# Graph attention on one Trainium2 core: u as the loaded operand of the heads' products, the table's rows as the moving one

## The chip, the core and the metric

The kernel runs on one core of one Trainium2 chip. The metric is the device time of one execution in microseconds (us). Three runs of the kernel before gave 2905.03, 2912.14 and 2910.83 us; the median is 2910.83 us. One more execution was profiled: 2910.45 us, of which 2908.7 us lie between its first and last instruction (the span). All times of single instructions come from that execution. The engines are TensorE (PE, whose weight loads have a row of their own, PEld), VectorE (DVE), ScalarE (ACT), GpSimd (POOL) and SyncE (SP, which issues transfers).

## The reference

Four graph layers run one after the other on 4096 nodes with 256 features; each is x = x + layer(relu(layernorm(x))). Layer 0 is an attention diffusion, layer 1 a graph convolution, layer 2 graph attention with four heads, layer 3 a product with the adjacency. The change is in layer 2:

```python
def _L2_gnn_ref(H, A, W, a_l, a_r):          # H: (4096, 256), A: (4096, 4096), sparse
    mask = A + eye(n) > 0
    Wh = (H @ W.T).reshape(n, 4, 64)
    score_l = einsum('nhd,hd->nh', Wh, a_l)
    score_r = einsum('nhd,hd->nh', Wh, a_r)
    e = score_l[:, :, None] + score_r.T[None, :, :]
    e = where(e >= 0, e, 0.2 * e)
    e = where(mask[:, None, :], e, -inf)
    alpha = softmax(e, axis=2)
    out = einsum('nhm,mhd->nhd', alpha, Wh).reshape(n, 256)
    return elu(out)
```

Each node averages the 64 features of its neighbours for every head, with weights that are a softmax over the neighbours. The adjacency has about four other neighbours to a row besides the node itself.

## The kernel before

The nodes are cut into 32 blocks of 128 targets (NB = 32, P = 128). An earlier part of the kernel has found, for each block, which source nodes have an edge into it: four chunks (CHUNKS = 4) of up to 128 sources, and half a chunk more, so that two neighbouring blocks share one spare chunk of 128. The block's own 128 nodes are a fifth chunk.

The layer before attention writes a table of one row for each node, 264 numbers wide (TW). For each of the four heads it holds 65 numbers (DK + 1): the 64 features times exp(0.2 score_r), and that factor itself, whose sum is the softmax's denominator. The last four numbers are exp(0.8 score_r). A second small array, steep_d, holds exp(0.8 score_l) of the targets. The weight of an edge, up to a factor that the division takes out, is then max(exp(0.8 score_l) exp(0.8 score_r), 1).

The attention stage works on one block in each pass of the loop at L2456 (b counts the passes), and on four parts of different blocks at the same time:

- load(b), L2363: SP issues the targets' factors and the block's own table rows; POOL issues four indirect gathers of table rows (every second block one more for the spare chunk). The pool of the table rows has five buffers.
- entries(b, k), L2379: for chunk k, ACT (L2394) and in some cases DVE (L2396) multiply the four heads' target factors by the sources' factors, 128 x 128 each, and DVE (L2397) takes the maximum with 1 and multiplies by the mask. The result is u: sources in the partitions, targets along the free axis. u has two buffers.
- attend(b - 1, h), L2401: for head h, TensorE sums over the sources in six matmuls, five chunks of 128 sources and the spare half chunk of 64 (L2407 and L2415). Each fp32 matmul shows as two passes in the trace, each with a weight load. The loaded operand is the 65 columns of the table's rows, the moving operand is u with 128 columns. The sums come out in the PSUM tile acc with the 65 numbers in the partitions and the targets along the free axis.
- attended(b - 2), L2423, copies acc to SBUF (ACT, tile sums), and turned(b - 2), L2427, transposes it by four TensorE transposes into the PSUM tile po, now with the targets in the partitions. divided, risen and elu (L2432 to L2453) divide by the denominator, apply elu and add to x.

Six passes behind, class Projection (third) prepares layer 3 for block o = b - 6: normalise (ACT L2238, two transposes L2243 on TensorE), turned (DVE L2248), product (two fp32 matmuls L2254 with 256 moving columns) and store (ACT L2265, SP L2266).

The order of work on DVE, ACT and TensorE is written out by hand in the loop: the instructions of each of these engines run as the lines stand. On TensorE a pass is: attend(b - 1, 0), the four transposes of turned(b - 2), the two transposes of normalise(o), the product of o - 1, then attend(b - 1, 1), (b - 1, 2) and (b - 1, 3). When the last block has been attended, the passes that are left finish elu and layer 3's projection. Then comes a small check (L2508 writes its verdict) and the last layer, whose gathers wait for the table that L2266 stores.

Of the kernel before, what the change touches and what calls it, by code (L numbers as in the profile page):

```python
# [63 lines left out]
F32 = mybir.dt.float32  # L64
# [12 lines left out]
P = 128  # L77
# [5 lines left out]
HEADS = 4  # L83
DK = D // HEADS
# [581 lines left out]
def fast_layers(  # L666
# [21 lines left out]
    nc = tc.nc  # L688
# [18 lines left out]
    ident = const.tile([P, P], F32, name="ident")  # L707
# [188 lines left out]
    def spare_index(table, b):  # L896
        at = CHUNKS * NB + b // 2
        return table[:, at : at + 1]
# [15 lines left out]
    def side(b):  # L914
        return slice(b % 2 * (P // 2), (b % 2 + 1) * (P // 2))
# [13 lines left out]
    wk = layer0.enter_context(tc.tile_pool(name="wk", bufs=2))  # L929
    ps = layer0.enter_context(tc.tile_pool(name="ps", bufs=2, space=PSUM))  # L930
# [1266 lines left out]
    class Projection:  # L2197
# [48 lines left out]
        def turned(self, b):  # L2246
            ht = self.wk.tile([P, DC, P], F32, name="ht")
            nc.vector.tensor_copy(ht, self.tiles[b])  # L2248
            self.tiles[b] = ht
# [22 lines left out]
    with ExitStack() as st:  # L2272
        adj_pool = st.enter_context(tc.tile_pool(name="gcnadj", bufs=6))
        sm = st.enter_context(tc.tile_pool(name="gcnsm", bufs=4))
        wk = st.enter_context(tc.tile_pool(name="gcnwk", bufs=3))
        ps = st.enter_context(tc.tile_pool(name="gcnps", bufs=2, space=PSUM))
# [27 lines left out]
        with tc.manual_schedule(engines=MANUAL):  # L2304
            for b in range(NB + LAG + 3):
# [21 lines left out]
                if b < NB:  # L2327
                    acc = ps.tile([P, D], F32, name="acc")
# [24 lines left out]
    with ExitStack() as st:  # L2353
        tab_pool = st.enter_context(tc.tile_pool(name="gattab", bufs=5))
        u_pool = st.enter_context(tc.tile_pool(name="gatu", bufs=2))
        sm = st.enter_context(tc.tile_pool(name="gatsm", bufs=4))
        wk = st.enter_context(tc.tile_pool(name="gatwk", bufs=3))
        ps = st.enter_context(tc.tile_pool(name="gatps", bufs=2, space=PSUM))
        third = Projection(sm, wk, ps, w_last, to_table(wk, v_d[1]), 2)
        state = [{} for _ in range(NB)]  # L2360
        LAG = 6

        def load(b):  # L2363
            t = state[b]["targets"] = tab_pool.tile([P, HEADS, P], F32, name="targets")
            nc.sync.dma_start(t, steep_d[b : b + 1].to_broadcast([P, HEADS, P]))
            tab = state[b]["tab"] = tab_pool.tile([P, CHUNKS + 1, TW], F32, name="tabg")
            nc.sync.dma_start(tab[:, CHUNKS, :], table_d[b * P : (b + 1) * P, :])
            if b % 2 == 0:
                t = state[b]["targets_x"] = tab_pool.tile([P, HEADS, P], F32, name="targets_x", bufs=3)
                for r in range(2):  # L2370
                    nc.sync.dma_start(
                        t[side(r)], steep_d[b + r : b + r + 1].to_broadcast([P // 2, HEADS, P])
                    )
                state[b]["tab_x"] = tab_pool.tile([P, TW], F32, name="tabg_x", bufs=3)
                gather(state[b]["tab_x"], table_d, spare_index(column, b))
            for k in range(CHUNKS):
                gather(tab[:, k, :], table_d, main_index(column, k, b))

        def entries(b, k):  # L2379

            s = state[b]
            if k > CHUNKS:
                if b % 2:
                    return
                u = s["u_x"] = u_pool.tile([P, HEADS, P], F32, name="u_x")
                t, factors, mask = s["targets_x"], s["tab_x"], masks_x[:, b // 2 : b // 2 + 1, :]
            else:
                if k == 0:
                    s["u"] = u_pool.tile([P, CHUNKS + 1, HEADS, P], F32, name="u")
                u, t, factors, mask = s["u"][:, k], s["targets"], s["tab"][:, k], masks[:, b, k : k + 1, :]  # L2390
            for h in range(HEADS):
                by = factors[:, HW + h : HW + h + 1]
                if h < HEADS - 1 or k % 3 == 0:
                    nc.scalar.mul(u[:, h, :], t[:, h, :], by)  # L2394
                else:
                    nc.vector.tensor_scalar(u[:, h, :], t[:, h, :], by, None, op0=ALU.mult)  # L2396
            nc.vector.scalar_tensor_tensor(  # L2397
                u, u, 1.0, mask.to_broadcast([P, HEADS, P]), op0=ALU.max, op1=ALU.mult
            )

        def attend(b, h):  # L2401

            s = state[b]
            if h == 0:
                s["acc"] = ps.tile([DK + 1, HEADS, P], F32, name="acc")
            for k in range(CHUNKS + 1):
                nc.tensor.matmul(  # L2407
                    s["acc"][:, h, :],
                    s["tab"][:, k, h * (DK + 1) : (h + 1) * (DK + 1)],
                    s["u"][:, k, h, :],  # L2410
                    start=(k == 0),
                    stop=False,
                )
            shared = state[b - b % 2]
            nc.tensor.matmul(  # L2415
                s["acc"][:, h, :],
                shared["tab_x"][side(b), h * (DK + 1) : (h + 1) * (DK + 1)],
                shared["u_x"][side(b), h, :],
                start=False,
                stop=True,  # L2420
            )

        def attended(b):  # L2423
            t = state[b]["sums"] = wk.tile([DK + 1, HEADS, P], F32, name="sums")
            nc.scalar.copy(t, state[b]["acc"])

        def turned(b):  # L2427
            po = state[b]["po"] = ps.tile([P, HEADS, DK + 1], F32, name="po")
            for h in range(HEADS):
                nc.tensor.transpose(po[:, h, :], state[b]["sums"][:, h, :], ident[: DK + 1, : DK + 1])  # L2430

        def divided(b):  # L2432
            s = state[b]
            rden = sm.tile([P, HEADS, 1], F32, name="rden")
            nc.vector.reciprocal(rden, s["po"][:, :, DK:])
            s["y"] = wk.tile([P, HEADS, DK], F32, name="y")
            nc.vector.tensor_tensor(
                s["y"], s["po"][:, :, :DK], rden.to_broadcast([P, HEADS, DK]), op=ALU.mult
            )

        def risen(b):
            s = state[b]
            s["below"] = wk.tile([P, D], F32, name="below")
            nc.scalar.activation(s["below"], s["y"].rearrange("p h d -> p (h d)"), AF.Exp)

        def elu(b):

            s, xo = state[b], xr[:, b, :]
            y = s["y"].rearrange("p h d -> p (h d)")
            below = s["below"]  # L2450
            nc.vector.scalar_tensor_tensor(xo, y, 0.0, xo, op0=ALU.max, op1=ALU.add)
            nc.vector.scalar_tensor_tensor(xo, below, 1.0, xo, op0=ALU.min, op1=ALU.add)
            third.stats(b)  # L2453

        with tc.manual_schedule(engines=MANUAL):
            for b in range(NB + LAG + 2):  # L2456
                o = b - LAG
                entered, summed, turning, ended = (0 <= b - k < NB for k in range(4))
                if entered:
                    load(b)  # L2460
                if turning:
                    attended(b - 2)
                if summed:
                    attend(b - 1, 0)
                if turning:
                    turned(b - 2)
                if 0 <= o < NB:
                    third.normalise(o)
                if 0 <= o - 1 < NB:
                    third.product(o - 1)  # L2470
                if ended:
                    elu(b - 3)
                if entered:
                    entries(b, 0)
                    entries(b, 1)
                if 0 <= o < NB:
                    third.turned(o)
                if summed:
                    attend(b - 1, 1)
                    attend(b - 1, 2)  # L2480
                if entered:
                    entries(b, 2)
                if turning:
                    divided(b - 2)
                if 0 <= o + 1 < NB:
                    third.shifts(o + 1)
                if entered:
                    for k in range(3, CHUNKS + 2):
                        entries(b, k)
                if turning:  # L2490
                    risen(b - 2)
                if 0 <= o - 2 < NB:
                    third.store(o - 2)
                if summed:
                    attend(b - 1, 3)
# [16 lines left out]
    with ExitStack() as st:  # L2512
        adj_pool = st.enter_context(tc.tile_pool(name="lastadj", bufs=6))
        wk = st.enter_context(tc.tile_pool(name="lastwk", bufs=3))
        ps = st.enter_context(tc.tile_pool(name="lastps", bufs=2, space=PSUM))
        for b in range(NB):
# [7 lines left out]
            acc = ps.tile([P, D], F32, name="acc")  # L2524
# [69 lines left out]
```

## Time and profile before

| what | us |
|---|---|
| runs of the kernel, median (lowest to highest) | 2910.83 (2905.03 to 2912.14) |
| the profiled execution | 2910.45 |
| its span | 2908.7 |
| first and last matmul pass of the attention heads (start) | 2454.6 and 2702.9 |
| verdict stored, last layer's first load (start) | 2714.7 and 2715.8 |
| passes of L2407 and L2415, all blocks | 1280 and 256 |

In the whole span PE is busy 2523.0 us, DVE 2312.7, ACT 1976.6 and POOL 1098.0. These are sums over stages that have different limits, so what matters here is the stretch from 2454 to 2715 us. The profile also gives the clock that TensorE was granted; it is either full or half, and changes in steps of 3.41 us. Its mean over the span is 0.921.

### The profile page before, as it was taken

The numbers are of one execution on the slowest core, as the hardware profiler recorded it, in microseconds if no ns is written. First come the engines' busy times: TensorE is split into PE (matmuls) and PEld (weight loads), VectorE is DVE, ScalarE is ACT, GpSimd is POOL, SyncE is SP. The second block draws the span as 40 slices with busy tenths as digits, with TensorE's granted clock in tenths as the row PEclk, the third lists the DMA queues.
The fourth block names the chain that finished last, engine by engine and source line by source line (L and its number), as shares of the span: only waits on it lengthen the run. The fifth ranks groups of instructions, "written<-read, shape, count | busy, mean of one in ns | idle before, by whom it ended". The sixth has DMA issues, their size and how long they took to land. (4 is left out here: it accounts for less than half of the span.)

```text
span 2908.7 us, 43850 instructions
## 1 busy us (share of the span) xinstructions
PE 2523.0 (87%) x12359; PEld 1850.5 (64%) x12359; DVE 2312.7 (80%) x9516; ACT 1976.6 (68%) x3289; POOL 1098.0 (38%) x1152
## 2 busy tenths in 40 slices
PE   5769999999999884699999999999895776999777
PEld 4537777777777762467676766677773554788444
DVE  4799999999999866898989879999964765888200
ACT  2689999999999634887888878788520123999100
POOL 3200000000000001488888554344425752764476
PEclk7779999999999996899999999999996887999887
DMA  7611222222222113244444433334337653654576
GB/s 254 222 55 59 92 69 87 89 69 91 80 75 89 40 40 103 64 126 126 122 136 118 134 111 102 99 117 123 101 98 227 209 165 104 173 164 121 160 210 183
DMA packets 227371, 349.57 MB, mean 120 GB/s; under 512 B 34727, under 2 KB 160172, under 8 KB 227116
## 3 DMA queue, kind: packets, MB, share of 16 engines
q1 hardware_dynamic: 185820, 237.70, 25.7%
q0 software_dynamic: 40320, 108.72, 13.6%
q8 instruction: 101, 1.65, 0.2%
q14 instruction: 154, 1.26, 0.1%
q10 hardware_dynamic: 976, 0.23, 0.0%
HBM read 280.22 MB, written 66.28 MB: 119 GB/s over the span
## 5 line engine op out<-in xcount | busy, mean ns | idle before, releaser
L1269 ACT ACTIVATE unread<-e,next_pair 128x4096 uint8<-128x4096 f32 (+1 forms) x320 | 859.5, 2686 | 160.9 <-DVE next_pair L1365 109.0
L1619 PE MATMUL pa<-va,at 128*128 128x256 f32 x2048 | 495.2, 387 | 0.0
L1619 PE MATMUL pa<-h,at 128*128 128x256 f32 x2048 | 469.0, 379 | 0.1
L1619 PEld LDWEIGHTS pa<-va,at 128*128 128x128 f32 x2048 | 376.4, 193 | 65.4 <-issue 21.6
L1619 PEld LDWEIGHTS pa<-h,at 128*128 128x128 f32 x2048 | 376.6, 190 | 45.3 <-issue 0.5
L1483 DVE MAX8 best<-near 128x8 f32<-128x256 f32 x1024 | 394.6, 415 | 0.1
L1610 ACT COPY at<-pat 128x512 f32<-128x512 f32 x512 | 284.0, 577 | 135.3 <-PE pat L1604 135.1
L1236 PE MATMUL pl<-kt,qb 64*128 64x512 f32 x1024 | 280.4, 657 | 91.3 <-ACT e L1250 88.4
L1604 PE MATMUL pat<-ident,e 128*128 128x128 f32 x2048 | 305.0, 279 | 51.2 <-DVEq L1543 25.1
L1604 PEld LDWEIGHTS pat<-ident,e 128*128 128x128 f32 x2048 | 240.0, 142 | 139.1 <-DVEq L1543 47.8
L1485 POOL COPY eighth<-best 128x16 f32<-128x16 f32 x64 | 47.1, 736 | 722.7 <-DVE best L1483 711.7
L1250 ACT ACTIVATE e<-pl,minus_guess 128x1024 f32<-128x1024 f32 x256 | 284.3, 1125 | 26.8 <-PE pl L1236 26.7
L1475 DVE SCALAR_TENSOR_TENSOR near<-e,end_hi 128x4096 f32<-128x4096 f32 x64 | 286.6, 4477 | 0.1
L1535 DVE SCALAR_TENSOR_TENSOR e<-e,end_t 128x4096 f32<-128x4096 f32 x64 | 286.2, 4472 | 0.2 <-issue 0.2
L889 POOL DMA_INDIRECT vg<-v_d,column x256 | 243.4, 951 | 91.0 <-issue 67.7
L920 PE MATMUL acc<-vg,ac 128*128 128x256 f32 x640 | 215.9, 489 | 66.3 <-DMA vg<-v_d,column 29.6
L920 PEld LDWEIGHTS acc<-vg,ac 128*128 128x128 f32 x640 | 146.9, 247 | 132.1 <-issue 59.8
L1236 PEld LDWEIGHTS pl<-kt,qb 64*128 64x128 f32 x1024 | 89.8, 194 | 195.7 <-ACT e L1250 156.4
L889 POOL DMA_INDIRECT vg<-mixed_d,column x128 | 180.5, 1410 | 57.6 <-issue 32.4
L2407 PE MATMUL acc<-u,tabg 128*65 128x128 f32 x1280 | 170.2, 280 | 13.5 <-DVE u L2397 13.5
L889 POOL DMA_INDIRECT vg<-far_d,column x128 | 166.6, 1301 | 39.0 <-issue 38.1
L2394 ACT ACTIVATE u<-targets,tabg 128x128 f32<-128x128 f32 x544 | 162.1, 389 | 10.0 <-DMA targets_x<-steep_d 10.0
(608 smaller groups left out, 4427.7 us busy)
## 6 DMA issues: line engine op xcount, KB each, us to landing
adj<-in_adjt SPq DMA_DIRECT2D x128, 512.0 KB
ac<-adjc_d SPq DMA_DIRECT2D x64, 320.0 KB
adjc_d<-ac SPq DMA_DIRECT2D x32, 320.0 KB
vg<-v_d SPq DMA_DIRECT2D x64, 128.0 KB
targets<-steep_d SPq DMA_DIRECT2D x32, 256.0 KB
ac<-adjc_d SPq DMA_DIRECT2D x32, 256.0 KB
table_d<-tab SPq DMA_DIRECT2D x32, 132.0 KB
tabg<-table_d SPq DMA_DIRECT2D x32, 132.0 KB
```

Source lines behind the costliest of these rows:

```text
L889: nc.gpsimd.indirect_dma_start(out, None, rows, bass.IndirectOffsetOnAxis(ap=index, axis=0))
L920: nc.tensor.matmul(acc, ac[:, k, :], v[:, k, :], start=(k == 0), stop=False)
L1236: nc.tensor.matmul(pl[:, r, :], s["qb"][rows], kt[rows, j * 512 : (j + 1) * 512], start=True, stop=True,)
L1250: nc.scalar.activation(s["e"][:, j * 1024 : (j + 1) * 1024], pl.rearrange("p r c -> p (r c)"), AF.Exp, bias=minus_guess[:, b : b + 1], acc ...
L1269: nc.scalar.activation(unread[:, :width], s["e"][:, :width], func, bias=s["at"], scale=-1.0, accum_out=s["signs"] if func == AF.Sign else ...
L1475: nc.vector.scalar_tensor_tensor(near, s["e"], end["hi"][:, b : b + 1], s["e"], op0=ALU.is_lt, op1=ALU.mult, accum_out=s["low"])
L1483: nc.vector.max(best[:, k, :], near[:, k * (N // SEG) : (k + 1) * (N // SEG)])
L1535: nc.vector.scalar_tensor_tensor(s["e"], s["e"], last, s["e"], op0=ALU.is_ge, op1=ALU.mult, accum_out=s["held"])
L1604: nc.tensor.transpose(pt[:, k, :], s["e"][:, c * P : (c + 1) * P], ident)
L1610: nc.scalar.copy(at, s["pt", g])
L1619: nc.tensor.matmul(s["pa"], s["at", g][:, k, :], va[:, c, :D], start=(c == 0), stop=(c == NB - 1))
L2407: nc.tensor.matmul(s["acc"][:, h, :], s["tab"][:, k, h * (DK + 1) : (h + 1) * (DK + 1)], s["u"][:, k, h, :], start=(k == 0), stop=False,)
```

## The change

The two operands of the six matmuls change places. u is loaded (128 columns) and the table's rows move (65 columns), so the sums come out in po with the targets in the partitions. The copy attended and the four transposes turned are dropped, with the tiles acc and sums.

```diff
             if h == 0:
-                s["acc"] = ps.tile([DK + 1, HEADS, P], F32, name="acc")
+                s["po"] = ps.tile([P, HEADS, DK + 1], F32, name="po")
+            cols = slice(h * (DK + 1), (h + 1) * (DK + 1))
             for k in range(CHUNKS + 1):
                 nc.tensor.matmul(
-                    s["acc"][:, h, :],
-                    s["tab"][:, k, h * (DK + 1) : (h + 1) * (DK + 1)],
-                    s["u"][:, k, h, :],
-                    start=(k == 0),
-                    stop=False,
+                    s["po"][:, h, :], s["u"][:, k, h, :], s["tab"][:, k, cols], start=(k == 0), stop=False
                 )
             shared = state[b - b % 2]
             nc.tensor.matmul(
-                s["acc"][:, h, :],
-                shared["tab_x"][side(b), h * (DK + 1) : (h + 1) * (DK + 1)],
-                shared["u_x"][side(b), h, :],
-                start=False,
-                stop=True,
-            )
-
-        def attended(b):
-            t = state[b]["sums"] = wk.tile([DK + 1, HEADS, P], F32, name="sums")
-            nc.scalar.copy(t, state[b]["acc"])
-
-        def turned(b):
-            po = state[b]["po"] = ps.tile([P, HEADS, DK + 1], F32, name="po")
-            for h in range(HEADS):
-                nc.tensor.transpose(po[:, h, :], state[b]["sums"][:, h, :], ident[: DK + 1, : DK + 1])
+                s["po"][:, h, :], shared["u_x"][side(b), h, :], shared["tab_x"][side(b), cols], start=False, stop=True
+            )
...
                 if entered:
                     load(b)
-                if turning:
-                    attended(b - 2)
                 if summed:
                     attend(b - 1, 0)
-                if turning:
-                    turned(b - 2)
```

## The prediction

> **What bounds the kernel now.** I read the busy table of the stage first, then the instructions of one loop pass, then the rows that price the new operand order, last the granted clock. The stretches of 40 us in the middle of the attention stage show which engine sets the pace (columns: stretch, length, busy us and count of PE, PEld, DVE, ACT, POOL, then clock, DMA share, GB/s):
>
> ```profile
> 2520.00:2560.00 40.00, 40.00 (x302) 32.24 (x301) 34.76 (x89) 36.21 (x117) 26.59 (x27) 1.00 0.62 174
> 2560.00:2600.00 40.00, 40.00 (x303) 32.05 (x302) 35.30 (x89) 37.05 (x120) 25.56 (x27) 1.00 0.58 166
> ```
>
> PE has no idle time and the full clock. Over 2470 to 2690 us DVE is busy 194.2 and ACT 201.0 of 220 us. The transposes of L2430 start 7.72 us apart in this stretch, so a block costs PE 7.72, DVE 6.81, ACT 7.05 us. PE is the bound, the others are near.
>
> The timeline shows what PE does (start, length, engine, line):
>
> ```profile
> 2565.67 0.46 PE L2430 MATMUL po<-ident,sums 65*128 65x65 f32 x4
> 2565.97 0.39 PE L2243 MATMUL pt<-ident,h 128*128 128x128 f32 x2
> 2566.19 1.03 PE L2254 MATMUL pv<-w_last,ht 128*128 128x256 f32 x4
> ...
> 2568.60 1.07 PEld L2407 LDWEIGHTS acc<-u,tabg 128*65 128x65 f32 x10 [0.17 <-issue]
> 2568.60 1.31 PE L2407 MATMUL acc<-u,tabg 128*65 128x128 f32 x10
> ...
> 2569.84 0.19 PEld L2415 LDWEIGHTS acc<-u_x,tabg_x 64*65 64x65 f32 x2 [0.17 <-issue]
> 2569.84 0.43 PE L2415 MATMUL acc<-u_x,tabg_x 64*65 64x128 f32 x2
> ```
>
> A head is ten passes of 128 source rows and two of 64; at each change between them the next load waits 0.17 us. From 2568.60 to 2570.20 a head costs 1.594 us, four cost 6.38; the transposes add 0.25 (2573.39 to 2573.64, before L2243 follows), L2243 and L2254 the rest.
>
> **What is removed.** Per block 0.25 us of transposes on PE, inside the bound: gain 0.25. The 0.17 us wait ahead of them stays, since L2243 now follows the 64-row passes. The ACT copy (582 ns, L2425) lies beside PE: nothing while PE is the bound (0.58 a block if ACT were), and ACT falls to 6.47 us a block. No engine waits on a new thing: po is written one loop pass earlier than it is divided, as acc was. On SP only the order of two loads in the stage's first blocks is exchanged; nothing is added to any queue.
>
> **What the swap costs at full clock.** Loads and passes exchange sizes: 128 columns loaded, 65 moved. The rows that price it:
>
> ```profile
> 2574.78 1.25 PE L2407 MATMUL acc<-u,tabg 128*65 128x128 f32 x10
> 63.79 0.97 PEld L1051 LDWEIGHTS pst<-halves,near 128*128 128x128 f32 x8
> 125.06 1.62 PEld L1051 LDWEIGHTS pst<-halves,near 128*128 128x128 f32 x7 [0.52 <-issue]
> 2573.39 0.33 PEld L2430 LDWEIGHTS po<-ident,sums 65*128 65x128 f32 x4 [0.17 <-issue]
> ```
>
> The first: ten passes with 128 moving columns, (1.25 - 0.272) / 9 = 0.109 us each; the load of 65 hides. L1051 loads 128 fp32 columns and moves two: at full clock (0.97 - 0.19) / 7 = 0.111 us, at half clock (1.62 - 0.333) / 6 = 0.2145. So the load alone then sets the pace, and the new passes, of the same load and 65 moving columns (half of 0.107 us), cost 0.111 each, not half. The low bound is the last row, 0.063 us a pass with 128 columns loaded and 65 moved, but in a transposition, one pass instead of two, whose load is shorter (L2243 shows the same 0.143 us as here; an fp32 load of 128 columns shows 0.190). The high bound is load and move in turn, 0.111 + 0.054. I take L1051, since it has the very load. The restart after each change of rows keeps its length: load 0.107 instead of 0.054, pass 0.054 instead of 0.107. Head: ten follow-on passes at +0.0025 plus some ns at the two restarts, about +0.034 us; four heads +0.14. Net at full clock 0.14 - 0.25 = -0.11 us a block.
>
> **What it costs through the clock.** Here is the decisive term. Windows on the 3.41 us grid on which the clock changes:
>
> ```profile
> 123.65:127.07 3.42, 3.42 (x11) 2.39 (x11) 2.98 (x11) 3.12 (x6) 0.00 (x0) 0.50 0.50 181
> 127.07:130.48 3.41, 3.41 (x11) 2.38 (x11) 2.85 (x22) 1.86 (x4) 0.00 (x0) 0.50 0.47 154
> 1113.52:1116.93 3.41, 3.23 (x21) 2.13 (x19) 1.83 (x8) 0.14 (x1) 0.00 (x0) 1.00 0.63 205
> 1116.93:1120.35 3.42, 0.00 (x0) 0.00 (x0) 3.08 (x12) 0.00 (x0) 0.00 (x0) 0.50 1.00 201
> 2458.37:2461.79 3.42, 3.03 (x12) 2.31 (x13) 2.86 (x8) 3.42 (x13) 2.50 (x4) 0.50 0.69 167
> 2461.79:2465.20 3.41, 3.41 (x16) 2.56 (x14) 2.11 (x4) 1.61 (x6) 2.80 (x3) 0.50 0.62 182
> 2465.20:2468.61 3.41, 3.41 (x26) 2.63 (x26) 0.00 (x0) 1.25 (x4) 2.49 (x4) 1.00 0.54 147
> ```
>
> The first two have PE busy throughout, half of it in L1051's loads, and the clock stays at half. The third has PE busy 3.23 us with sixteen two-column passes, and the clock falls behind it. So neither busy time nor loads count. I added up, for every window of the trace, the share in which columns move (0.107 us for 128 at full clock, 0.213 at half). At full clock it fell after every window below 0.37 and after none above 0.44; at half it rose after none below 0.74 and after all above 0.86. In the stage itself, 2458.37 holds 11 moving passes of 0.213 (0.71) and stays, 2461.79 about 14 (0.88) and releases the full clock.
>
> The stage begins at half clock and will be left there: a new pass moves 0.108 of each 0.2145 us, a share of 0.51 at best and 0.44 with the changes of rows. Half-clock heads cost as much as now by the same exchange of sizes: 2460.06 to 2463.00 = 2.94 us. Not before layer 3's matmuls start, behind attend(6, 0), is there more that moves: two transposes of 0.213 and four passes of 0.427, 2.13 us in one piece. A window that holds this piece and 1.28 us of heads reaches (2.13 + 1.28 x 0.5) / 3.41 = 0.81, between the bounds; a block offers such a window with a chance of (3.41 - 2.13) / 3.41 = 0.38. I take one block until the clock rises, with none and all as ends.
>
> At full clock a window inside the heads has a share of 12 x 0.054 / 1.628 = 0.40, again between the bounds. There, windows with 6 to 8 passes lost the clock 21 times in 28, those with 10 or more kept it three times in three; as if each pass counted some ns more than its columns. A new window holds 25 passes, so I take it that the clock is kept, with its loss as the rival.
>
> [...]
>
> **The sum.** (1) From 2465.65 to 2503.9, the start of the sixth group of transposes, are 22 heads at full clock now, 38.25 us; at half they take 22 x 2.94 = 64.7: +26.4. POOL, ACT and DVE have slack there. (2) One block more with layer 3's matmuls at half clock: 4 x 2.94 + 2.13 = 13.9 against 7.72: +6.2. (3) 24 blocks at full clock: -2.7. (4) The tail: after the last head PE waits 0.97 us for the copy and runs the transposes, at the head of the chain that reaches 2714.7; without them about -1.2. Sum +28.7, on the profiled execution's 2910.45 (0.4 below the median): **2939 us**. With no or four blocks in (2) it is 2933 to 2958; with the 5 us by which the runs of before differ, the forecast's own range is 2928 to 2963.
>
> ```profile
> 2703.30 0.58 ACT L2425 COPY sums<-acc 65x512 f32<-65x512 f32 x1 [3.82 <-PE acc L2415]
> 2703.93 0.33 PEld L2430 LDWEIGHTS po<-ident,sums 65*128 65x128 f32 x4 [0.97 <-ACT sums L2425]
> ```
>
> **Rivals.** A, the clock does not last: windows inside the heads at 0.40 lose it and most of the stage runs at half. For it: the 21 of 28. Against: the windows with many passes. If never regained: 26.4 + 25 x 6.2 + some 5 for a tail at half clock = +186, 3097; with a quarter of the blocks at full clock some 40 less, 3055. About 3075.
> B, the clock is as now (busy time decides): -0.11 x 30 - 1.2 = -4.6, 2906. Against it: the windows above.
> C, faster: loads of 128 columns partly hide, passes near L2430's 0.063, and the clock comes as now. PE falls by 48 x 0.046 = 2.2 us to below DVE, which then sets 6.81 + 0.05: -0.86 x 30 - 1.2 = -27, 2883. It decides once a pass costs under 0.092 us (PE at DVE's 6.85). Against: L1051 in both clocks.
>
> **How the numbers follow.** Forecast 0.55, A 0.25, B 0.12, C 0.08. The first two hold 0.8, so the range runs from 2925 to 3100; B and C are left out. Changes under 0.3% (8.7 us) can't be told from none: slower 0.80, same 0.11 (B), faster 0.09 (C and B's lower end).
>
> **What would show it.** Passes of the heads start 0.111 us apart at full and 0.2145 at half clock; the granted clock is half from 2454 until layer 3's matmuls run, some 2530 to 2545, then full. If the clock is full by 2466, term (1) falls; if it keeps changing after 2545, A holds; if passes stand 0.06 to 0.09 apart, the load was mispriced.

## The result, and the profile after

The changed kernel takes 3067.73 us (3062.09 to 3068.87) against 2911.05 us: 1.0539 times the kernel before, with a 95% interval of 1.0519 to 1.0558. The profiled execution has a span of 3066.2 us against 2908.7, 157.5 us more.

The place is the attention stage alone. From the first to the last matmul pass of the heads it takes 409.6 us (2450.7 to 2860.2) instead of 248.4. The stage starts 3.9 us earlier for reasons that lie ahead of it (in a second trace of the kernel before it starts 9.3 us earlier with the same code), and the last layer takes 194.0 us in both: 161.2 - 3.9 + 0.2 behind the heads = 157.5.

Busy time of the changed kernel in 40 us stretches of the stage (columns as in the prediction):

```profile
2580.00:2620.00 40.00, 40.00 (x160) 36.32 (x159) 20.32 (x51) 18.74 (x61) 13.94 (x15) 0.50 0.36 101
2700.00:2740.00 40.00, 40.00 (x237) 36.23 (x237) 28.70 (x71) 30.49 (x100) 21.47 (x23) 0.80 0.52 144
2780.00:2820.00 40.00, 40.00 (x157) 36.08 (x158) 19.02 (x49) 18.24 (x60) 8.37 (x10) 0.50 0.17 47
```

PE is busy all the time, as before, but at a granted clock of 0.50, and its passes in 40 us have fallen from 302 to 160. DVE and ACT have fallen from about 35 to 20 us. From 2500 to 2690 us the trace puts 70.3 us of DVE's waits for u down to ACT and names nothing for 94.4 us of ACT's; that both wait in the end for PE to free one of the two buffers of u is inferred, from PE alone having no idle time. A reader who looks at busy shares alone would see no difference on PE. The chain that ended last, from the page of the changed kernel, agrees:

```profile
PE 15%; POOL 2%; DMA 2%; issue 1%; DVE 0%; ACT 0%; POOLq 0%; SPq 0%; ACTq 0%; DVEq 0%
```

The chain on the page of the kernel before (PE 1%) can be followed back only to 2707 us, behind the heads; now it runs through the heads' passes. Their timeline, at half clock and at full clock:

```profile
2573.69 2.39 PE L2408 MATMUL po<-tabg,u 128*128 128x65 f32 x10
2576.02 0.69 PE L2412 MATMUL po<-tabg_x,u_x 64*128 64x65 f32 x2
2576.63 2.39 PE L2408 MATMUL po<-tabg,u 128*128 128x65 f32 x10
...
2704.98 1.33 PE L2408 MATMUL po<-tabg,u 128*128 128x65 f32 x10
2706.24 0.43 PE L2412 MATMUL po<-tabg_x,u_x 64*128 64x65 f32 x2
2706.60 1.33 PE L2408 MATMUL po<-tabg,u 128*128 128x65 f32 x10
2704.98 1.19 PEld L2408 LDWEIGHTS po<-tabg,u 128*128 128x128 f32 x10
```

A head costs 2.94 us at half clock and 1.62 at full clock. The loads at full clock are (1.19 - 0.19) / 9 = 0.111 us apart: a pass moves half the columns and takes as long as before (0.109 us), so by these rows the load sets the pace (in the runs below with 72, 80 and 128 moved columns and the same load the passes of a train start 0.111 to 0.112 us apart too). What makes the difference is how long each clock lasts. I take the distance from one block's first 64-row pass to the next block's (differences are taken before rounding):

| block distances | after, us | before, us | difference |
|---|---|---|---|
| 6 without layer 3's matmuls, half clock | 70.9 | 44.1 | +26.8 |
| 20 with them, all at half clock, 13.79 each | 275.9 | 154.5 | +121.3 |
| 3 in which the clock changes (9.71, 10.74, 11.01) | 31.5 | 23.2 | +8.3 |
| 2 at full clock, 7.53 each | 15.1 | 15.5 | -0.4 |
| behind the last of these, to the start of the last head's last pass | 11.1 | 6.3 | +4.8 |

So at full clock the new order was a little faster (7.53 against 7.72), but only two whole blocks had it. In this trace, as in that of the kernel before, every stretch of full or of half clock is a whole number of 3.413 us long. Windows of the changed kernel on that grid show how the full clock comes and goes:

```profile
2526.23:2529.64 3.41, 3.41 (x13) 2.81 (x12) 2.14 (x5) 2.78 (x10) 2.59 (x3) 0.50 0.85 223
2693.48:2696.89 3.41, 3.41 (x15) 3.06 (x13) 3.06 (x9) 2.23 (x7) 2.07 (x3) 0.50 0.69 198
2696.89:2700.31 3.42, 3.42 (x26) 3.10 (x25) 1.89 (x6) 0.00 (x0) 0.00 (x0) 1.00 0.13 37
...
2713.96:2717.37 3.41, 3.41 (x27) 3.07 (x26) 2.75 (x7) 2.07 (x8) 1.74 (x2) 1.00 0.46 129
2717.37:2720.79 3.42, 3.42 (x14) 3.06 (x13) 3.18 (x9) 3.42 (x13) 2.73 (x3) 0.50 0.85 212
2720.79:2724.20 3.41, 3.41 (x27) 3.14 (x27) 3.06 (x8) 1.76 (x6) 0.84 (x2) 1.00 0.21 59
2724.20:2727.61 3.41, 3.41 (x16) 3.17 (x15) 1.57 (x5) 2.64 (x10) 1.67 (x2) 0.50 0.40 116
```

The third number from the end is the clock of the window. I added up the share in which columns move, as in the prediction. It is an estimate from the distance of passes in this trace: at full clock passes of 512 columns start 0.429 us apart (L1646), which is 0.107 for 128, and at half clock passes of 256 start 0.427 apart (L2254), 0.213 for 128. The first window has 0.76 and is not followed by full clock; the second has 0.76 too and is. The third (0.40) keeps it, 2713.96 (0.40) loses it, 2717.37 (0.80, with layer 3's matmuls) is followed by one window at full clock, and 2720.79 (0.40) loses it again. PE is busy in all of them.

### The profile page after: what moved, and what is told of

The parts are those of the page before. It is cut to its first block, busy times and chain, and to the rows that moved or that the text cites. A ratio compares the mean times of both kernels' runs of the same rounds, so it can differ in the third digit from the quotient of the medians.

```text
span 3066.2 us, 43621 instructions
## 1 busy us (share of the span) xinstructions
PE 2675.4 (87%) x12231; PEld 2019.6 (66%) x12231; DVE 2316.1 (76%) x9516; ACT 1964.5 (64%) x3257; POOL 1088.4 (35%) x1152
## 5 line engine op out<-in xcount | busy, mean ns | idle before, releaser
L2408 PE MATMUL po<-tabg,u 128*128 128x65 f32 x1280 | 286.8, 403 | 13.5 <-DVE u L2397 13.5
L1485 POOL COPY eighth<-best 128x16 f32<-128x16 f32 x64 | 40.3, 630 | 724.2 <-DVE best L1483 713.2
L2408 PEld LDWEIGHTS po<-tabg,u 128*128 128x128 f32 x1280 | 271.4, 313 | 30.1 <-issue 12.4
L2397 DVE SCALAR_TENSOR_TENSOR u<-u,masks 128x512 f32<-128x512 f32 x160 | 110.7, 692 | 156.1 <-ACT u L2394 134.7
```

The costliest lines, as they stand in the source:

```text
L2408: nc.tensor.matmul(s["po"][:, h, :], s["u"][:, k, h, :], s["tab"][:, k, cols], start=(k == 0), stop=False)
```

## The experiments

The theory after the result: in this kernel the granted clock follows the share of time in which columns move through PE, as estimated above. 65 columns behind a load of 128 give 0.40 inside the heads at full clock, behind which it was lost at 2717.37 and 2724.20 us (and kept at 2700.31), and 0.44 at half clock, behind which no window of the stage rose to full. The main rival: the new operand order is slow in itself, by its loads or because a head's work has grown. The first four runs fell on a chip on which the kernel before took 3129.16 us (other stages are slower there: the attention stage's gathers begin at 2612.0 us in the run with 128 columns, at 2445.9 in the trace of the kernel before), the others on chips with 2911 us; each ratio is to the kernel before on its own chip.

**128 columns moved.** Of the table's rows 128 columns are moved where 65 are needed; the other sums are overwritten or not read.

```diff
+        MOVED = 128
...
-                s["po"] = ps.tile([P, HEADS, DK + 1], F32, name="po")
-            cols = slice(h * (DK + 1), (h + 1) * (DK + 1))
+                s["po"] = ps.tile([P, HEADS, P], F32, name="po")
+            low = min(h * (DK + 1), TW - MOVED)
+            to = h * P + low - h * (DK + 1)
+            sums = s["po"].rearrange("p h d -> p (h d)")[:, to : to + MOVED]
+            cols = slice(low, low + MOVED)
...
```

The matmuls then write `sums`.

> The operands stand as in the changed kernel (u loaded, 128 columns), but each pass moves 128 columns of the table's rows instead of 65; the other 63 sums are thrown away. Loads, number of passes and everything else stay. Theory (the granted clock follows the share of time in which columns move): at half clock a head moves 12 x 0.213 of 2.95 us, 0.87, so full clock is granted at some 2465 us as in the kernel before, a pass stays at 0.111 us because the load sets the pace, a block costs 7.53 us, and the time is 2900 to 2912 us although more work is done. Rival (the new order is slow in itself, by its longer loads, or PE work counts): 3068 us or more, half clock in most of the stage.

Measured: 1.0018 (0.9999 to 1.0038) instead of 1.0539, some 4 us of 2911 above what was expected. The first full clock, from 2631.2 us, was lost at 2638.0, when PE had almost nothing to do (a share of 0.06); the second lasted from 2658.5 us to the end of the stage. Nearly twice the moved columns with the same loads takes the loss away (1.0018 instead of 1.0539): the rival falls. A block took 7.9 us and not the 7.53 that I expected. The heads show where the time is:

```profile
2700.36 1.38 PE L2413 MATMUL po<-tabg,u 128*128 128x128 f32 x10
2701.67 0.49 PE L2415 MATMUL po<-tabg_x,u_x 64*128 64x128 f32 x2
2702.08 1.38 PE L2413 MATMUL po<-tabg,u 128*128 128x128 f32 x10
```

A head is 1.72 us instead of 1.62. Inside the trains the passes still start 0.111 to 0.112 us apart; what has grown lies at the changes of rows, with 1.31 us instead of 1.26 from the first of the ten passes to the first of the two, and 0.41 instead of 0.36 from there to the next ten. My reading, an estimate from these four distances: at each change the load of 128 and the pass of 128 both stand open, where the two kernels have one long and one short.

**80 columns moved** (the same edit with MOVED = 80).

> As the run with 128 moved columns, but with 80. Theory: at full clock a window inside the heads has a share of 12 x 0.0667 / 1.63 = 0.49, above the 0.44 over which the clock was never lost in the kernel before, so once full it stays full; at half clock the heads alone have 0.55 and cannot raise it, a window that holds layer 3's matmuls whole reaches 0.85 and can. So half clock up to 2530 us and some blocks more, then full to the end: 2935 to 2965 us, the course that my forecast described for 65 columns. Rival (a clock once low stays low in this operand order): about 3068 us.

Measured: 1.0079 (1.0050 to 1.0107), some 23 us of 2911 and just below the range expected. Busy time in this run (its stage begins later, on the slower chip):

```profile
2680.00:2720.00 40.00, 40.00 (x158) 35.91 (x158) 20.43 (x52) 19.96 (x64) 15.36 (x17) 0.50 0.33 90
2720.00:2760.00 40.00, 40.00 (x285) 36.08 (x284) 33.10 (x86) 32.07 (x105) 23.50 (x24) 1.00 0.57 153
2760.00:2800.00 40.00, 40.00 (x285) 36.02 (x284) 34.79 (x89) 34.36 (x112) 25.14 (x26) 1.00 0.59 167
```

This is the course that I had forecast for 65 columns: half clock until layer 3's matmuls have run for some two blocks, then one rise at 2719.9 us, and full clock to the end of the stage, with blocks of 7.6 us.

**A warm start.** Five matmuls of 512 moving columns behind the first head, results unused:

```diff
                 if summed:
                     attend(b - 1, 0)
+                if b == 1:
+                    spare = ps.tile([P, 512], F32, name="spare", bufs=1)
+                    for _ in range(5):
+                        nc.tensor.matmul(spare, ident, xr[:, 0:2, :].rearrange("p b d -> p (b d)"), start=True, stop=True)
```

> The changed kernel (65 moved columns) with five more fp32 matmuls of 512 moving columns behind the first head, whose result is not used; they take 6 to 9 us and raise the clock to full before the heads begin. It parts the two steps of my forecast: is the clock kept in the heads (my forecast), or lost in windows with a share of 0.40 (rival A of the prediction)? Kept: full clock from 2465 us to the end of the stage, about 2906 + 8 = 2914 us. Lost: full clock for one to six windows, then half until layer 3's matmuls or longer, 3045 to 3080 us.

Measured: 1.0519 (1.0479 to 1.0558). The clock rose at 2628.2 us and was lost at 2635.0. This is not quite the test that I meant. The window before the loss:

```profile
2631.58:2634.99 3.41, 2.82 (x20) 2.30 (x19) 1.13 (x3) 0.00 (x0) 2.80 (x3) 1.00 0.35 89
2634.99:2638.40 3.41, 0.54 (x2) 0.57 (x2) 0.69 (x1) 0.00 (x0) 2.66 (x3) 0.50 0.52 132
```

PE had run ahead and stood idle, with a share of 0.30; ACT had nothing to multiply, and POOL was still issuing gathers. Four later losses in this run are clean: the clock came back for one window each at 2792.0, 2802.2, 2979.7 and 2990.0 us and was lost after shares of 0.40, with PE busy throughout. The run with 65 columns further down repeats the question without the filler.

**128 columns, in pairs.** Heads 0 and 1, and 2 and 3, have their 64-row matmuls side by side:

```diff
...
-                    attend(b - 1, 0)
+                    attend_chunks(b - 1, 0, True, False)
...
-                    attend(b - 1, 1)
-                    attend(b - 1, 2)
+                    attend_spare(b - 1, 0, False, True)
+                    attend_spare(b - 1, 1, True, False)
+                    attend_chunks(b - 1, 1, False, True)
+                    attend_chunks(b - 1, 2, True, False)
+                    attend_spare(b - 1, 2, False, True)
...
-                    attend(b - 1, 3)
+                    attend_spare(b - 1, 3, True, False)
+                    attend_chunks(b - 1, 3, False, True)
```

Here attend_chunks holds the ten passes of 128 rows of a head and attend_spare the two of 64.

> As the run with 128 moved columns, and the 64-row matmuls of two heads stand side by side (heads 0 and 1, heads 2 and 3), so that PE changes between 128 and 64 rows 4 times a block instead of 8. Theory: each pair of changes that falls away saves two waits of 0.09 us and most of two exposed loads of 0.107, some 0.3 us, 0.6 a block; PE falls from 7.53 to about 6.95 us a block, DVE's 6.81 lies just under it: 2882 to 2895 us. Rival (DVE or the u buffers already set the pace at 7.53): the same as the run with 128 moved columns.

Measured: 0.9944 (0.9924 to 0.9963). Blocks fell from 7.9 to 7.2 to 7.5 us: the four changes of rows are worth the 0.6 us that were expected, from the higher start.

**The kernel before, once more, and with pairs** (the same edit on acc).

> The kernel before, unchanged, for a trace on the same chip as the runs beside it. Blocks of the attention stage 7.7 us apart, full clock from the third block on.

> The kernel before (table loaded, u moving, copy and transposes kept), with the 64-row matmuls of heads 0 and 1 and of heads 2 and 3 side by side. Theory (the changes between 128 and 64 rows cost PE some 0.15 us each, and PE is the bound): 4 changes fewer a block, 0.6 us, block 7.1 us, 0.993 to 0.996 of the time before. Rival (DVE or ACT or the u buffers hold the block at 7.7): 1.000.

Measured: the kernel before took 2901.54 us in this one run, with blocks of 7.72 us and full clock from 2454.5 us, 9 us behind the start of the first head. With pairs 0.9955 (0.9939 to 0.9971), blocks of 7.2 to 7.4. ACT is busy 38.6 to 39.1 of 40 us there and has little left.

**72 columns behind a warm start of four blocks with 128.** This asks where the border lies. The rest is as in the run with 128 columns, with moved(b) in place of MOVED.

```diff
+        def moved(b):
+            return P if b < 4 else 72
```

> u loaded, 128 columns moved in the first four blocks and 72 in the others, no pairs. A window inside the heads has a share of 12 x 0.060 / 1.63 = 0.44 at full clock, at the upper edge of what lost the clock in the kernel before. Share theory: kept in most windows, 0.998 to 1.010 of the time before; seven columns fewer (65, share 0.40) lost it within two windows in the run with the warm start. Rival (what counts is something else than the columns, so 72 is like 65): lost in the first blocks with 72, 1.03 to 1.06.

Measured: 0.9974 (0.9957 to 0.9990), a little better than expected. The clock was full from 2462.2 to 2711.4 us without a break; every window inside the heads with 72 columns had a share of 0.42 to 0.46 and kept it.

**65 columns behind eight blocks with 128**, the clean test of whether the clock is kept.

> u loaded, 128 columns moved in the first eight blocks, 65 in the other 24; no pairs. The clock is full when the blocks with 65 begin, and layer 3's matmuls are there in each of them. Kept once full (my forecast): 0.997 to 1.001 of the time before. Lost at a share of 0.40 in windows inside the heads (as the run with the warm start): the clock falls in the first or second of these blocks and comes back now and then, 1.025 to 1.05.

Measured: 1.0423 (1.0402 to 1.0444). Full clock until 2517.0, 3.4 us once more from 2523.8, and then half until 2728.6:

```profile
2480.00:2510.00 30.00, 29.73 (x206) 25.54 (x204) 26.44 (x67) 25.37 (x83) 24.04 (x23) 1.00 0.64 167
2540.00:2580.00 40.00, 40.00 (x159) 36.28 (x158) 20.91 (x51) 20.50 (x66) 13.85 (x15) 0.50 0.34 91
2680.00:2720.00 40.00, 40.00 (x158) 36.15 (x158) 20.92 (x51) 20.28 (x66) 13.90 (x15) 0.50 0.33 91
```

All four losses followed windows with shares of about 0.40. Next to it the run with 72 columns at the same place:

```profile
2540.00:2580.00 40.00, 40.00 (x287) 36.35 (x286) 35.80 (x91) 35.50 (x118) 24.95 (x27) 1.00 0.61 166
```

Seven columns more a pass decide between half and full clock here.

**65 columns in pairs.** Here the columns stay and the waits between them shrink.

> As the run beside it, with the 64-row matmuls in pairs. The columns and passes are the same, but PE waits less at changes of rows: the heads of a block take some 6.0 instead of 6.5 us, so the share in which columns move is 48 x 0.0542 / 6.0 = 0.43 instead of 0.40. Share theory: above the 0.41 at which 65 columns lost the clock and near the 0.42 to 0.45 at which 72 kept it, so kept in most blocks: 0.993 to 1.005. Rival (65 columns lose the clock whatever the waits): as the run beside it.

Measured: 1.0052 (1.0033 to 1.0072), just above the upper end that I expected, and far below the 1.0423 of the run without pairs. Windows of 0.42 to 0.45 kept the clock many times and lost it once (0.43). One longer loss, 2626.4 to 2681.0 us, begins as follows (the window before it, then PE's timeline):

```profile
2622.99:2626.40 3.41, 3.05 (x25) 2.77 (x25) 3.17 (x9) 1.99 (x7) 1.42 (x2) 1.00 0.52 138
...
2623.66 2.22 PE L2415 MATMUL po<-tabg,u 128*128 128x65 f32 x18
2626.24 0.58 PE L2415 MATMUL po<-tabg,u 128*128 128x65 f32 x2 [0.36 <-DVE u L2397]
```

With a wait of 0.36 us for DVE the window has a share of 0.37, and four blocks at 13 us followed. So in these two runs it is the share that counts, not the number of columns in a pass: the same 65 columns kept the clock in windows of 0.42 to 0.45, where PE waits less between them, and lost it at about 0.40 without pairs. And it is a fragile place to stand. All thirteen traces agree on this: of 682 windows at full clock between the first and the last head, 17 were followed by half clock, and all 17 have shares of 0.43 or less; of the windows below 0.39 none kept it.

**128, then 80 columns, in pairs**, with four and with eight blocks of 128 at the start.

> u loaded, 128 columns of the table moved in the first four blocks, which raise the clock, and 80 in the others, which keep it; the 64-row matmuls in pairs. Theory: full clock from the third block to the end as in the run with 128 columns and pairs, and blocks of 7.0 to 7.15 us, against 7.2 to 7.5 there: 0.990 to 0.994 of the time before, below both kernels. If 80 columns could not keep the clock: over 1.02.

Measured: 0.9955 (0.9938 to 0.9971), above what was expected. The clock was lost from 2496.1 to 2509.7 us, after a window with a share of 0.26 in which PE waited for DVE; the block took 12.85 us.

> As the run with 128 and 80 columns and pairs, with 128 columns in the first eight blocks instead of four. In that run one window with a share of 0.26, while PE waited for DVE in the fifth block, took the clock for 13.7 us. Theory: with 128 columns until layer 3's matmuls run, it is not lost or comes back at once, and some 5 us are gained: 0.992 to 0.995 of the time before.

Measured: 0.9936 (0.9923 to 0.9950), as expected: 2892.88 us against 2910.76. Full clock from 2456.5 to 2695.5 us, blocks with 80 columns of 7.06 to 7.7. It is faster than both kernels of this case, and about as fast as the kernel before with pairs, whose interval overlaps with it. DVE is busy 36.8 of 40 us in it, PE 39.3.

## Why the prediction was wrong

It gave 2939 us; the time lies near its rival A (3055 to 3097, taken as 3075). Step by step:

- **The bound** was right: PE, in a stage where the other engines are near.
- **What is removed and what the swap costs at full clock** was right in kind, with L1051's load as the price. Passes stand 0.111 us apart; a block fell by 0.19 us (7.72 to 7.53) instead of 0.11.
- **"The stage begins at half clock and will be left there"** was right, and so was its price: +26.8 us for the blocks without layer 3's matmuls, against +26.4; 2.94 us a head; 13.79 us a block with them, against 13.9.
- **"So I take it that the clock is kept, with its loss as the rival"** is the step that failed. I had put the share inside the heads at 0.40, between the bounds, where 21 of 28 windows with few passes had lost the clock, and let three windows with 10 or more passes decide. Over the changed kernel, the warm start and the run with 65 columns behind 128, of 13 windows inside the heads with shares of 0.397 to 0.413 and 25 or 26 passes each, 11 were followed by half clock. Many passes in a window did not keep it. The 21 of 28 foretold these 11 of 13 better than the three did.
- **"I take one block until the clock rises"** failed as well. From the first window that could have done it (2526.2) to the rise at 2696.9 went twelve blocks. I had treated each block as a draw of its own with a chance of 0.38. But a block of 13.79 us is 4.04 windows long, so layer 3's matmuls move by only 0.14 us a block against the grid (13.79 - 4 x 3.413): they start 1.26 us behind one of its edges at 2541.13 us and 2.80 behind one at 2692.86, and in each of the twelve blocks from the one to the other the next edge cuts them. After the loss at 2527.2 the run with 65 columns behind 128 waited fourteen blocks in the same way. Nor was there one share from which it rose: rises were seen from 0.75 on in these runs, and 0.77, 0.78 and, in the first blocks of the run with 128 columns in pairs, 0.83 went by without one.
- **The tail** gained nothing: 12.0 us against 11.8, for without copy and transposes it began at half clock (0.50 up to 2867.6 us, against 1.00 in the whole of the tail before).

Together the two failed steps turn the +3.5 us that terms (2) and (3) gave for the blocks with layer 3's matmuls into the +129.2 of the table.

## What to carry to other kernels

Before exchanging the operands of a matmul, add up the share of time in which columns will move, not only the pace of the passes: at the same pace of 0.111 us and with PE busy throughout, this kernel lost its clock at a share of 0.40 (65 columns) and kept it at 0.44 (72). Where a share comes out as near as that to one that lost the clock, treat the loss as the likely case. Blocks are not separate draws either: here they came every 13.79 us against windows of 3.413 us, 4.04 to a block, and twelve of them gave the same answer. Moving columns whose sums are not needed was the cheaper way here (72 for 65: 0.9974 instead of 1.0423), with the passes 0.111 to 0.112 us apart in both.

## What the runs showed of the hardware that was not expected

- More work was faster: with 72 moved columns instead of 65, and nothing else changed in the kernel but the length of the start with 128, the ratio was 0.9974 instead of 1.0423.
- The border is narrow in these traces. Inside the heads 0.397 to 0.413 lost the clock 11 times in 13; with 72 columns shares of 0.42 to 0.46 never did. What decides inside these few hundredths (0.40 was kept twice, 0.43 lost once) is open.
- A single wait was dear: 0.36 us of waiting for DVE was followed by 54.6 us at half clock.
- Four changes between 128 and 64 rows a block are worth 0.4 to 0.6 us: 7.7 to some 7.3 us a block in the kernel before, 7.9 to some 7.3 with 128 columns.
